# Fewer, wider segments in the second top-p search of a two-layer graph kernel

## The chip, the cores and the metric

The kernel runs on one core of one Trainium2 chip, in one launch, all in fp32. The metric is the device time of that launch in microseconds (us). TensorE is called PE below (PEld is its weight load), VectorE DVE, ScalarE ACT, GpSimd POOL and SyncE SP.

## The reference, cut to what matters

N is 2708 nodes with 256 features; adj is a sparse 2708 x 2708 matrix.

```python
x = layernorm(x + relu(concat([x, adj @ x]) @ weight + bias))          # layer 0
# layer 1
R = adj + eye(N);  R = R / R.sum(-1)
Xf = Xa = x;  Z = 0
for n in range(2):
    q = Xa @ W1.T @ W2.T;  k = Xa @ W3.T
    probs = softmax(q @ k.T)                     # N x N
    # of each row, keep the largest entries until their sum reaches TOP_P = 0.9
    idx = argsort(-probs);  sp = probs[idx];  cs = cumsum(sp)
    A = probs * (cs - sp < 0.9 at its place);  A = A / A.sum(-1)
    Xf = R @ Xf;  Xa = A @ Xa
    Z = Z + Xf @ U1[n].T + Xa @ U2[n].T
x = layernorm(x + layernorm(x + Z) * ln_g + ln_b)
```

Nothing is sorted over all 2708 entries of a row in the kernel. What it needs of a row is the threshold: the smallest entry that is kept.

## The kernel before, in words

The rows are cut into NB = 22 blocks of 128, the last (EDGE) with 20 rows. The work goes in three stages: layer 0; step 1 of the attention, together with a compaction of adj into at most 128 x 7 nonzero columns a block; and step 2 of the attention together with both products with R over the compacted columns. The change lies in step 2.

**Step 2, one block.** PE makes the logits in three parts (`logits`, L507); ACT takes their exponentials into a row buffer `e` (`exps2`, L844) and adds them up; DVE sums the three parts into the row's total z (`begin_search`, L852). Then a level is sought below which the threshold lies. The first level comes from a sum of square roots; for each level ACT goes over the row twice (`try_act`, L966 and L969, Relu and Sign with a running sum), which gives the mass and the number of entries above the level. `next_level` (L977) turns these into the next level with three constants of STEPS, and `last_level` (L1003 to L1013) picks one of two levels with the constant FEW. A row's level is thus a guess, made so that few entries stand between it and the threshold.

DVE finishes the row in this order:

- `below_level` (L1023): one pass that sets entries at or above the level to zero, into `low`, and adds up the rest;
- `candidates` (L1030): one MAX8 for each of NS2 segments of SEG2 elements of `low`, which gives the 8 largest of each segment, 160 candidates in `cand`;
- `in_order` (L1039, L1042): MAX8 and MATCH_REPLACE8 in turn, until TOP2 = 48 candidates stand in falling order in `srt`;
- `threshold` (L1058 to L1078): a running sum over these, the first that reaches the mass still needed, and how many entries equal to it are to be kept;
- `mark` (L1083): four MATCH_REPLACE8 of a quarter row, which mark these equal entries;
- `mask` (L1088): one pass that keeps what is above the threshold, in `e`.

PE then turns the masked row in six groups of up to four 128 x 128 transposes (`turn`, L527), ACT copies each group out of PSUM (L530), and PE multiplies (`products`, L564).

**The order of the work.** It is written out by hand as a loop over 24 periods with six slots each. In period `per` ACT tries the levels of block per + 1 and takes the exponentials of block per + 2; DVE does the level, `low` and candidates of block per, and the sorting, threshold, marks and mask of block per - 1; PE multiplies block per - 2, and does its share of the product with R (`r_units`, L749) in between. DVE's six slots are the generator `vector_slots`; `turns` deals out the steps of two generators alternately, so that a step which needs the result of the one before has others in front of it. The lines on which the edit acts are:

```python
run_all(turns((part_of_it(order, 7) if b else None, 1), (levels, 1)))   # slot 0
below_level(a)                                                          # slot 1
run_all(turns((order, 1), (part_of_it(cands, 8) if a else None, 2)))    # slot 2
run_all(turns((limits, 1), (cands, 2)))                                 # slot 3
mark(b, 0); mark(b, 1)                                                  # slot 4
mark(b, 2); mark(b, 3); run_all(begin); mask(b)                         # slot 5
```

Here a is block per and b is block per - 1. In the last two periods one or both are missing.

At the end of the program flags are added up: a row whose level was too low, whose threshold was not among the sorted candidates, or whose segment held more than 8 of the wanted entries sets one. If any is set, a branch runs `general_path`, which does the whole of layer 1 anew by another method.

Of the kernel before, what the change touches and what calls it, by code (L numbers as in the profile page):

```python
# [21 lines left out]
CH = 512  # L22
SEG = 170
NS = 16
SEG2 = 136
NS2 = 20
TOP1 = 64
TOP2 = 48
WS = 4

GUESS = 2.76141059
STEPS = ((0.93339875, 14.44678062, 82.55022771), (0.98700001, 8.00991560, 128.06811957))
FEW = 20.0
TOP_S = 0.8999
TIE_EPS = 1.5e-5
KS = 7
# [14 lines left out]
def gnn_two_layer_kernel(ctx: ExitStack, tc: tile.TileContext, N, xT_d, x_d, adj_d, w0_d, b0_d,  # L53
# [29 lines left out]
    assert N % 2 == 0 and NB % 2 == 0 and N * 2.0 ** -15 < 0.09 and DC == 2 and DA == 64  # L83
    assert SEG * (NS - 1) + 8 <= N <= SEG * NS == SEG2 * NS2 and N >= SEG2 * (NS2 - 1) + 8
    assert NB == 3 * KS + 1 and CW == P and CAP % 8 == 0 and N < NB * P
# [63 lines left out]
def fast_path(ctx, tc, c, flags, fint, xT_d, x_d, w0_d, b0_d, w1_d, w2_d, w3_d, u1_d, u2_d, g_d, b_d):  # L149
# [417 lines left out]
    def seg_max(dst, src, p, step, width):  # L567
        for i in range(NS):
            w = min(width, N - SEG * i) if step == SEG else width
            nc.vector.max(dst[:p, i * 8:(i + 1) * 8], src[:p, i * step:i * step + w])  # L570

    def put_in_order(dst, n, cand, p):

        spare = small.tile([P, NS2 * 8], FP, tag="spare", name="spare", bufs=1)[:, :cand.shape[1]]
        src = cand
# [11 lines left out]
    def extract1(t):  # L587
        p = rows(t)
        e = es[t % 4]
        cand = small.tile([P, NS2 * 8], FP, tag="cand", name="cand", bufs=2)[:, :NS * 8]  # L590
        seg_max(cand, e, p, SEG, SEG)
# [385 lines left out]
    def next_level(b, k):  # L977
        keep, slope, down = STEPS[k]
        nc.scalar.activation(b.kept, b.l[k], AF.Copy, scale=keep + TOP_P * slope, bias=-down)
        nc.scalar.activation((b.l1, b.l2)[k], b.u[k], AF.Identity, bias=b.kept, scale=-slope)  # L980
        if k:
            nc.scalar.activation(b.few, b.l1, AF.Copy, scale=TOP_P, bias=-FEW)

# [5 lines left out]
    def try_dve(b, k):  # L989
# [5 lines left out]
        if k == 0:  # L995
            keep, slope, down = STEPS[0]
            nc.vector.tensor_scalar(b.kept, b.l0, keep + TOP_P * slope, -down, op0=ALU.mult, op1=ALU.add)
# [20 lines left out]
    def below_level(b):  # L1018
# [5 lines left out]
                                       accum_out=bulk[:p, 2, t:t + 1])  # L1024
        b.cand = small.tile([P, NS2 * 8], FP, tag="cand", name="cand", bufs=2)

    def candidates(b):
        p = b.p
        for i in range(NS2):
            nc.vector.max(b.cand[:p, 8 * i:8 * i + 8], low[:p, SEG2 * i:SEG2 * (i + 1)])  # L1030
            yield

    def in_order(b):
        p = b.p
        b.srt = small.tile([P, TOP1 + 1], FP, tag="srt", name="srt", bufs=3)
        spare = small.tile([P, NS2 * 8], FP, tag="spare", name="spare", bufs=1)
        src = b.cand
        for i in range(0, TOP2, 8):
            nc.vector.max(b.srt[:p, i:i + 8], src[:p])  # L1039
            yield  # L1040
            if i + 8 < TOP2:
                nc.vector.match_replace(spare[:p], b.srt[:p, i:i + 8], src[:p], -3.0e38)  # L1042
# [3 lines left out]
    def threshold(b):  # L1046


        t, p = b.t, b.p
        s = b.srt[:p, :TOP2]  # L1050
        sc = small.tile([P, 3 + 2 * WS], FP, tag="sc", name="sc", bufs=3)
# [4 lines left out]
        x = sums  # L1056
        q_ = small.tile([P, TOP1], FP, tag="qs", name="qs", bufs=1)[:p, :TOP2]
        nc.vector.scalar_tensor_tensor(need, b.z, TOP_P - 1.0, below, op0=ALU.mult, op1=ALU.add)  # L1058
        nc.vector.tensor_tensor_scan(x[:p, 1:TOP2 + 1], s, s, 0.0, op0=ALU.add, op1=ALU.bypass)
        yield  # L1060
        nc.vector.scalar_tensor_tensor(q_, x[:p, 1:TOP2 + 1], need, s, op0=ALU.is_ge, op1=ALU.mult)
        yield
# [668 lines left out]
```

## Time and profile before

| what | us |
|---|---|
| median of 3 runs | 1310.96 |
| lowest and highest run | 1307.9, 1312.36 |
| the profiled execution | 1361.88 |
| its span, first to last instruction | 1360.1 |
| step 2, first `below_level` to the end | 779.0 to 1360.1 |

The profile is of one execution, at a mean granted TensorE clock of 0.969. All durations and places are on that execution's own time line. The rows of the edited lines on full blocks are: L1030, MAX8 of 128 x 136, 420 times, mean 286 ns; L1039, MAX8 of 128 x 160, 126 times, mean 316 to 319 ns; L1042, MATCH_REPLACE8 of 128 x 160, 105 times, mean 309 ns. Step 1 has the same operations in other widths: L570, MAX8 of 128 x 170, mean 320 ns; L577, MAX8 of 128 x 128, mean 284 to 295 ns; L579, MATCH_REPLACE8 of 128 x 128, mean 275 ns. A mean there is from the start of an instruction to the end of its write; the next instruction may start before that.

### The profile page before, as it was taken

What the parts mean: (1) busy time and instruction counts of PE and PEld (TensorE: products, weight loads), DVE (VectorE), ACT (ScalarE), POOL (GpSimd) and SP (SyncE); (2) the same over time, 40 slices, a digit from 0 to 9 for tenths busy, and PEclk for the clock granted to TensorE, in tenths of its full rate; (3) what the DMA queues carried; (4) which work ended last, traced back from release to release, by engine and by line L of the source; (5) the groups of instructions that cost most, each with busy time, mean ns of one, the idle gap of its engine ahead of it and who ended that gap; (6) DMA issues with size and microseconds to landing.
All of it is one profiled execution on the core that took longest, in us unless ns stands there. A gap on an engine that the chain in (4) does not pass through costs nothing.

```text
span 1360.1 us, 18883 instructions
## 1 busy us (share of the span) xinstructions
PE 1250.1 (92%) x5764; PEld 895.5 (66%) x5764; DVE 998.1 (73%) x3406; ACT 733.8 (54%) x1337; POOL 635.2 (47%) x594
## 2 busy tenths in 40 slices
PE   8999999988999999999997959999996999999985
PEld 6877877733567777666774727766664776666763
DVE  2544545866888888877840469878877899999995
ACT  1011011035455565555553577877786898998931
POOL 1000000014554533777563177777743668888850
PEclk9999999989899999999998969999998999999997
DMA  6554545513222110232222245645543444554541
GB/s 186 163 176 155 166 155 160 165 54 117 81 92 67 55 57 10 89 94 95 69 73 74 68 150 157 188 140 175 172 111 109 148 159 143 171 181 151 169 111 33
DMA packets 101993, 166.27 MB, mean 122 GB/s; under 512 B 17394, under 2 KB 74358, under 8 KB 101882
## 3 DMA queue, kind: packets, MB, share of 16 engines
q1 hardware_dynamic: 75596, 108.91, 24.7%
q0 software_dynamic: 20544, 51.17, 13.6%
q10 hardware_dynamic: 5742, 4.89, 1.3%
q8 instruction: 48, 0.79, 0.2%
q14 instruction: 63, 0.52, 0.1%
HBM read 130.87 MB, written 34.03 MB: 121 GB/s over the span
## 4 chain that ended last, share of the span: by engine, by line
PE 67%; ACT 19%; DVE 6%; issue 4%; another core or an unknown queue 2%; DMA 0%; ACTq 0%; DVEq 0%
PE acc L564 22%; PE acc L257 15%; PE lg L507 8%; PE tr L527 5%; PE misc L749 5%; ACT e L969 4%; ACT e L966 3%; ACT e L844 3%; ACT wT L530 3%; PE acc L651 2%; PE acc L462 2%; PE misc L426 2%; PE misc L392 2%; PE acc L672 2%
## 5 line engine op out<-in xcount | busy, mean ns | idle before, releaser
L530 ACT COPY wT<-tr 128x512 f32<-128x512 f32 (+2 forms) x258 | 131.7, 518 | 254.7 <-PE tr L527 153.3
L564 PE MATMUL acc<-ya,wT 128*128 128x256 f32 (+1 forms) x924 | 234.6, 394 | 18.8 <-ACT wT L530 12.1
L564 PE MATMUL acc<-x,wT 128*128 128x256 f32 (+1 forms) x924 | 234.6, 393 | 13.2 <-ACT wT L530 12.9
L719 POOL DMA_INDIRECT yg<-v_d,ix x154 | 190.1, 1234 | 79.4 <-issue 32.3
L564 PEld LDWEIGHTS acc<-x,wT 128*128 128x128 f32 (+1 forms) x924 | 167.2, 192 | 87.8 <-issue 40.6
L719 POOL DMA_INDIRECT yg<-yf_d,ix x154 | 192.6, 1250 | 62.3 <-issue 36.2
L564 PEld LDWEIGHTS acc<-ya,wT 128*128 128x128 f32 (+1 forms) x924 | 169.8, 193 | 75.6 <-issue 28.1
L257 PE MATMUL acc<-y,adj_t 128*128 128x257 f32 (+1 forms) x924 | 208.4, 381 | 0.0
L367 POOL DMA_INDIRECT adj_t<-in_adj,ix x154 | 170.3, 1106 | 51.4 <-issue 42.4
L749 PE MATMUL misc<-yg,adj_t 128*128 128x256 f32 (+1 forms) x704 | 183.5, 395 | 11.4 <-issue 6.6
L257 PEld LDWEIGHTS acc<-y,adj_t 128*128 128x128 f32 (+1 forms) x924 | 171.8, 189 | 32.7 <-issue 8.9
L507 PE MATMUL lg<-k,q 64*128 64x512 f32 (+3 forms) x528 | 151.9, 602 | 29.7 <-issue 11.2
L749 PEld LDWEIGHTS misc<-yg,adj_t 128*128 128x128 f32 (+1 forms) x704 | 125.7, 191 | 61.7 <-issue 31.2
L527 PE MATMUL tr<-ident,e 128*128 128x128 f32 (+2 forms) x946 | 147.0, 274 | 2.3 <-DVE e L1088 2.3
L527 PEld LDWEIGHTS tr<-ident,e 128*128 128x128 f32 (+2 forms) x946 | 113.6, 139 | 41.5 <-issue 17.6
L334 POOL DMA_DIRECT2D part_d<-e x1 | 0.6, 576 | 286.2 <-DVE e L333 286.2
L966 ACT ACTIVATE e<-e,st 128x2708 f32<-128x2708 f32 (+1 forms) x43 | 113.6, 2641 | 0.1
L570 DVE MAX8 cand<-e 128x8 f32<-128x170 f32 (+1 forms) x352 | 87.6, 318 | 32.7 <-ACT e L514 15.4
L969 ACT ACTIVATE e<-e,st 128x2708 f32<-128x2708 f32 (+1 forms) x42 | 110.9, 2641 | 0.1
L439 ACT COPY x1T<-tr 128x256 f32<-128x256 f32 (+1 forms) x22 | 8.0, 364 | 186.6 <-PE tr L438 186.6
L1030 DVE MAX8 cand<-w 128x8 f32<-128x136 f32 (+1 forms) x440 | 106.2, 285 | 0.0
L507 PEld LDWEIGHTS lg<-k,q 64*128 64x128 f32 (+1 forms) x528 | 39.3, 183 | 64.2 <-issue 35.6
(237 smaller groups left out, 1762.9 us busy)
## 6 DMA issues: line engine op xcount, KB each, us to landing
adj_t<-in_adj SPq DMA_DIRECT2D x44, 704.0 KB
adj_t<-adjc_d SPq DMA_DIRECT2D x44, 448.0 KB
adjc_d<-adj_t SPq DMA_DIRECT2D x22, 256.0 KB
base<-za_d SPq DMA_DIRECT2D x41, 128.0 KB
adjc_d<-adj_t SPq DMA_DIRECT2D x22, 192.0 KB
xt<-in_x ACTq DMA_DIRECT2D x21, 128.0 KB
x_d<-x SPq DMA_DIRECT2D x21, 128.0 KB
x1b_d<-xb SPq DMA_DIRECT2D x21, 128.0 KB
```

Source lines behind the costliest of these rows:

```text
L257: nc.tensor.matmul(acc[:p, :n], lhsT=halves[k // KH][:kw, k % KH, :p], rhs=y[:kw, k, :n], start=k == 0, stop=stop and k == NB - 1)
L367: nc.gpsimd.indirect_dma_start(out=a[:CW, i, :], out_offset=None, in_=adj_rows, in_offset=bass.IndirectOffsetOnAxis(ap=ix[:CW, m, i:i + 1] ...
L507: nc.tensor.matmul(lg[:p, h, :b - a], lhsT=q[o, t * P:t * P + p], rhs=keys[s][o, i, :b - a], start=True, stop=True)
L527: nc.tensor.transpose(tr[:kw, k % 4, :p], e[:p, k * P:k * P + kw], ident[:p, :p])
L530: nc.scalar.copy(wT[:, :full, :p], tr[:, :full, :p])
L564: nc.tensor.matmul(acc[:p, :D], lhsT=wT[:kw, k % 4, :p], rhs=y[:kw, k, :], start=k == 0, stop=k == NB - 1)
L570: nc.vector.max(dst[:p, i * 8:(i + 1) * 8], src[:p, i * step:i * step + w])
L719: nc.gpsimd.indirect_dma_start(out=y[:CW, i, :], out_offset=None, in_=rows_d, in_offset=bass.IndirectOffsetOnAxis(ap=ix[:CW, m, i:i + 1], ...
L749: nc.tensor.matmul(acc[:p, :D], lhsT=a[:kw, k, :p], rhs=y[:kw, k, :], start=k == 0, stop=k == CC)
L966: nc.scalar.activation(scr[:b.p, :N], e, AF.Relu, bias=b.nz, scale=b.l[k], accum_out=b.relu)
L969: nc.scalar.activation(scr[:b.p, :N], e, AF.Sign, bias=b.nz, scale=b.l[k], accum_out=b.sign)
L1030: nc.vector.max(b.cand[:p, 8 * i:8 * i + 8], low[:p, SEG2 * i:SEG2 * (i + 1)])
```

## The change

Step 2's candidates come from NS2 = 16 segments of SEG2 = 170 elements instead of 20 of 136, which is 128 candidates instead of 160, and TOP2 = 40 of them are put in order instead of 48. The constants by which the levels follow from one another are others. No function is edited; the loops and widths above follow from the constants. The row buffers stay 2720 elements wide (16 x 170 = 20 x 136), and a quarter row of `mark`, 680 elements, is four segments instead of five.

```diff
-SEG2 = 136
-NS2 = 20
+SEG2 = 170
+NS2 = 16
 TOP1 = 64
-TOP2 = 48
+TOP2 = 40
...
-STEPS = ((0.93339875, 14.44678062, 82.55022771), (0.98700001, 8.00991560, 128.06811957))
-FEW = 20.0
+STEPS = ((0.93305, 13.13978, 71.625), (1.02196, 8.0735, 138.42237))
+FEW = 18.8904
```

For a block, `candidates` issues 16 instead of 20 MAX8, `in_order` five MAX8 and four MATCH_REPLACE8 instead of six and five, and `threshold` the same operations on 40 and 128 elements instead of 48 and 160. In `vector_slots` slot 0 still takes seven steps of the sorting; two instead of four are left for slot 2, and eight instead of twelve candidate searches for slot 3.

## The prediction

> **What bounds the kernel now.** I read the page's busy shares first, then its chain of work, then the busy time by stage, then the chain and the timeline in two places: a steady period of step 2 and the end.
>
> ```profile
> PE 1250.1 (92%) x5764; PEld 895.5 (66%) x5764; DVE 998.1 (73%) x3406; ACT 733.8 (54%) x1337; POOL 635.2 (47%) x594
> PE 67%; ACT 19%; DVE 6%; issue 4%; another core or an unknown queue 2%; DMA 0%; ACTq 0%; DVEq 0%
> ```
>
> VectorE is busy for 73% of the span but holds 6% of the chain that ended last. The change edits VectorE alone, so the question is where that 6% lies. By stage (core, then length, then busy us of PE, PEld, DVE, ACT, POOL):
>
> ```profile
> 1151.56:1252.33 100.77, 95.08 (x443) 67.72 (x442) 94.35 (x343) 89.16 (x156) 83.36 (x73) 1.00 0.54 168
> 1252.33:1300.55 48.22, 44.35 (x219) 34.09 (x218) 46.27 (x166) 40.84 (x70) 39.91 (x36) 1.00 0.55 166
> 1300.55:1360.10 59.55, 39.30 (x221) 26.66 (x219) 45.14 (x146) 12.64 (x33) 11.71 (x12) 0.84 0.21 53
> ```
>
> The first row is four equal periods of 25.19 us. PE, DVE and ACT are all 88 to 94% busy, so busy time doesn't say which one sets the period. The chain and the timeline do (start, length, engine; in the timeline the idle time before is in brackets):
>
> ```profile
> 1190.24 0.48 ACT wT L530
> 1190.77 1.99 PE acc L564 x8
> ...
> 1199.03 1.99 PE acc L564 x8
> ...
> 1202.36 0.59 ACT wT L530
> ```
>
> ```profile
> 1194.66 0.16 DVE L852 TENSOR_REDUCE bulk<-st 128x1 f32<-128x3 f32 x1 [1.37 <-issue]
> 1202.36 0.59 ACT L530 COPY wT<-tr 128x512 f32<-128x512 f32 x1 [2.64 <-PE misc L749]
> ```
>
> The loop is ACT to PE to ACT: ACT's copy of turned weights releases eight matmuls, PE goes on to the next period's first transposes, ACT copies those after its only long pause, 2.64 us, and is then busy all period. No DVE piece stands in the chain from 779 to 1280 us. DVE pauses once a period, 1.36 us at L852, which sums what ACT's third exponential (L844, its accumulator read out at 1194.63) leaves. Its mask (L1088) ends at 1199.0; the transposes that need it start at 1201.73, so it is 2.7 us early. The second slack is larger than the first, so DVE work saved in a steady period becomes a longer pause at L852.
>
> The end is another matter. From L852 at 1270.18 to the end of the last mask at 1336.4 DVE has one pause, 0.11 us at L792, and the chain is on DVE from 1280.82:
>
> ```profile
> 1294.74 3.07 DVE e L1088 x2
> ...
> 1317.90 3.07 DVE e L1088 x2
> ...
> 1333.34 3.06 DVE e L1088 x2
> ...
> 1338.89 5.95 PE acc L550 x44
> ```
>
> ```profile
> 1321.11 0.63 PE L527 MATMUL tr<-ident,e 128*128 128x128 f32 x4 [2.28 <-DVE e L1088]
> ```
>
> No further exponentials are started there, ACT is busy for a fifth of the last stage, and PE waits 2.28 us for a mask. **Only here does saved DVE time shorten the run.**
>
> **What the Trainium skill says.** "Perfetto Trace Analysis", Optimizing Scalar/DVE Operations: a DVE operation on SBUF has about 60 ns of its own engine time, and the profiled latency is about twice the overhead, since the write acknowledgement overlaps the next instruction. So start-to-start time is the cost, not the listed mean. The trace agrees: 136 elements at 0.96 GHz ("VectorE: DVE Perf Modes", Specifications and errata table) and 60 ns give an estimate of 202 ns, and 20 MAX8 take (4.11 - 0.29)/19 = 201 ns each, though the row's mean is 286. The first page's section on the most-contended engine warns that matmul busy time is no measure of PE's distance from its limit; hence I go by pauses and the chain.
>
> ```profile
> 782.81 4.11 DVE L1030 MAX8 cand<-w 128x8 f32<-128x136 f32 x20
> 604.13 1.52 DVE L570 MAX8 cand<-e 128x8 f32<-128x170 f32 x6 [1.09 <-ACT e L514]
> 1321.82 0.32 DVE L1039 MAX8 srt<-spare 20x8 f32<-20x160 f32 x1
> 1322.58 0.32 DVE L1039 MAX8 srt<-spare 20x8 f32<-20x160 f32 x1
> 611.67 0.29 DVE L577 MAX8 srt<-spare 128x8 f32<-128x128 f32 x1
> 612.38 0.29 DVE L577 MAX8 srt<-spare 128x8 f32<-128x128 f32 x1
> ```
>
> **The change part by part**, for one row block. Step 1 already works with 170 and with 128 candidates, so its rows price the new shapes.
>
> *Candidates (L1030).* Before 20 x 0.203 = 4.06 us (0.201 alone, 0.205 between other steps). After 16 at 170 elements: step 1 has (1.52 - 0.32)/5 = 0.240, and 0.248 over a run of twelve; I take 0.244, 3.90 us. Gain 0.16 us; from 0.06 (at 0.250) to 0.27 (at 0.237).
>
> *Putting in order (L1039, L1042).* One MAX8, one MATCH_VALUE_LOAD and one MATCH_REPLACE8 fall away (six and five become five and four). Between other steps they occupy 0.23 + 0.29 = 0.52 us; with nothing between, as at 1321.82 to 1322.58, 0.76. The remaining nine are 32 elements narrower: 0.76 against step 1's 0.71 a pair gives 0.05 for each of 4.5 pairs, 0.22; by elements it would be 0.30. I take 0.25.
>
> *Threshold (L1058 to L1078).* Five operations on 40 instead of 48 and two on 128 instead of 160 save about 0.12 us by elements (bounds 0.05 and 0.2). But the steps are dealt out in turn: before, 4 sorting and 6 threshold steps had two candidate searches behind each; after, 2 and 4 have them, and L1071, L1073 lose their cover. Uncovered (block 21) L1071 to L1073 takes 0.34 and L1073 to L1075 0.24; covered, 0.22 and 0.12 to 0.19. Loss about 0.18 us (0.1 to 0.5, since L1061, L1064 and L1078 now and then take 0.65 to 0.75 in this trace).
>
> *Other constants.* They are immediates of the same instructions: no time. They do decide how many elements are left between level and threshold. Worked out with the formulas of L979, L980, L982 and L1003 to L1013 on the reference's input, the most any row needs is 34 elements (40 now kept) and 7 from one segment (8 kept), and no row's level lies past 0.9; so the branch to the general path stays untaken. Nothing is moved to another queue, and no DMA or semaphore wait on another engine is added.
>
> Sum for a covered block: 0.16 + 0.52 + 0.25 + 0.12 - 0.18 = 0.87 us; over 22 blocks some 19 us of DVE. For 19 of them the cover is DVE's own pause and the 2.7 us that the mask is early: nothing. After 1270.18 lie the sorting and threshold of blocks 19, 20 (covered, 0.87 each, with the searches of 20 and 21) and of 21 (no searches beside it: 0.76 + 0.25 + 0.12 = 1.13). Sum **2.87 us**. Does PE allow it? By the mask of block 20 it is 1.74, under PE's pause of 2.28. PE's own work for block 20 ends at 1335.2 and would end at 1333.5; the last mask would end at 1336.4 - 2.9 = 1333.5. Both are just met; PE is late next, so there is nothing beyond about 2.9 us. (The 0.11 us at L792 is put down to a matmul; if that holds, the 0.2 saved in front of it, in block 19's first sorting steps, is lost.)
>
> The profiled execution took 1361.88 us (span 1360.1), so 1359.0 is the sum against its own time. The median without profile is 1310.96, 51 us lower, with runs from 1307.9 to 1312.36; nothing in the end stage explains that difference, so I subtract the same 2.9: **1308.1 us**. That is 0.22%. About 0.3%, 3.9 us, is what a measurement of this kernel can tell from no change. The bounds (candidates 0.06 to 0.27, sorting 0.7 to 0.85, threshold -0.45 to 0.1) give 1 to 3.7 us.
>
> **The rivals.**
>
> *B, DVE is the bound in runs without profile.* If the ACT-PE loop is over 1.36 us shorter there, DVE sets every period and up to 19 us come off: 1292. For it: DVE is 94% busy, and plain runs are 51 us shorter. Against it: spread evenly, 51 us in 1361 is 0.94 us of a 25.19 us period, less than the pause; and the granted clock was already 1.00 in these periods, where the loop has least to gain. A partial form gives 4 to 10 us.
>
> *C, slower: stops that the trace puts down to no one.* In step 2 the chain has "another core or an unknown queue" at 796.3 (5.99 us), 810.2 (1.34), 907.7 (3.70), 989.4 (2.69), 1040.1 (4.54) and 1049.5 (0.97): 19.2 us, most of them before ACT instructions while DMA is heavy. 154 DVE instructions fewer move DVE against ACT and the transfers. Two further stops of the mean 3.2 us cost 6.4, less 2.9: 1314.5; at four, 1321. It decides from about seven added us. Against it: ACT's and PE's programs are unchanged, and the ACT-PE loop, not DVE, times them.
>
> *D, nothing comes out.* If the uncovered threshold steps cost 0.5 and PE or the gathered rows (PE waits 1.15 us for yg at 1312.65) hold the end: under 1 us, 1310.5.
>
> **How the numbers follow.** Main case 0.60: 1308.1, own range 1306.5 to 1310; with the scatter of medians I read it as within 0.3% for 0.44 of these and as faster for 0.16. B 0.22, faster. C 0.13, slower. D 0.05, within 0.3%. Faster 0.16 + 0.22 = 0.38, within 0.3% 0.44 + 0.05 = 0.49, slower 0.13. The range 1298 to 1314 takes in the partial form of B and leaves out its full form and the worse half of C.
>
> **What would show it.** Right: DVE's count falls by 154 to 3252; MAX8 at L1030 x352 near 320 ns; the pause at L852 in steady periods grows from 1.36 to about 2.2 while periods stay at 25.2; the stretch from the last L852 to the end of the last mask shrinks from 66.2 to about 63.4 us. Wrong: steady periods shorter than 25 us without a new clock (B), new unattributed stops on ACT or DVE (C), a PE pause before the last L544 that is released by matmuls (D).

## The result, and the profile after

The changed kernel takes **6518.32 us** (median of 6 runs, 6510.56 to 6522.13), the kernel before 1309.43 us (6 runs beside them, 1305.68 to 1312.36): a ratio of 4.9755, with a 95% interval from 4.9651 to 4.9858. The forecast was 1308.1 us, with a range from 1298 to 1314.

The page of the kernel after shows that a second program has run behind the first. Its lines are engine, busy us, share of the span and number of instructions, then the chain that ended last by engine, and the costliest group (count, busy us, mean ns, idle time before it):

```profile
span 6508.8 us, 37828 instructions
PE 2881.0 (44%) x11676; PEld 1998.5 (31%) x11676; DVE 5929.0 (91%) x8620; ACT 1347.3 (21%) x2298; POOL 749.3 (12%) x682
DVE 77%; PE 17%; ACT 3%; issue 2%; DMA 0%; SPq 0%; POOL 0%; DVEq 0%; ACTq 0%; POOLq 0%
L1516 DVE SCALAR_TENSOR_TENSOR scr<-e,cand 128x2708 f32<-128x2708 f32 (+1 forms) x1188 | 3630.1, 3056 | 49.7 <-ACT e L1495 4.1
```

L1516 stands in `general_path`. It has no row in the profile of before; here it runs 1188 times, which is 2 steps x 22 blocks x 27 passes of 3.06 us over whole rows, and is over half of the span. The chain is now on DVE for 77%.

Where the second program begins is seen in SP's queue and in the chain of waits (start, length, what):

```profile
1299.77 10.28 SPq L1424 DMA_DIRECT2D x<-x_d  x22
```

```profile
1297.88 0.42 DVE h L1190
1298.72 0.51 SPq L127
...
1310.48 7.08 DMA adj_t<-in_adj
...
1400.02 3.06 DVE scr L1516 x2
1403.18 3.06 DVE scr L1516 x2
```

L127 reads the sum of the flags. The last layer norm of the ordinary path (L1190) ends at 1298.3, where the kernel before would have been done but for its last stores; at 1299.77 L1424 loads x again for `general_path`. From there to the end are 6508.8 - 1299.8 = 5209.0 us, and the medians differ by 6518.32 - 1309.43 = 5208.9. **The loss is the branch at the end; none of it that could be seen lies in the search.**

Ahead of the branch the profile can be laid beside that of before. Busy time by stage (start and end, length, busy us of PE, PEld, DVE, ACT, POOL, granted clock, DMA share, GB/s), each stage at the same distance from the last L852 as before:

```profile
1099.95:1200.64 100.69, 95.01 (x442) 67.77 (x441) 91.08 (x313) 89.17 (x156) 82.32 (x73) 1.00 0.55 168
1200.64:1248.86 48.22, 44.36 (x219) 34.20 (x218) 45.39 (x151) 41.35 (x72) 39.66 (x36) 1.00 0.55 167
1248.86:1299.70 50.84, 39.23 (x221) 27.92 (x219) 43.67 (x134) 12.14 (x32) 10.90 (x12) 0.87 0.24 59
```

```profile
1142.95 0.16 DVE L852 TENSOR_REDUCE bulk<-st 128x1 f32<-128x3 f32 x1 [2.10 <-ACT e L844]
1150.66 0.59 ACT L530 COPY wT<-tr 128x512 f32<-128x512 f32 x1 [2.64 <-PE tr L527]
```

Four steady periods take 100.69 us where they took 100.77, though DVE is busy for 91.08 and not 94.35. The timeline says why: DVE's pause at L852 has grown from 1.37 to 2.10 us, and ACT's pause of 2.64 us stands as it was.

### The profile page after: what moved, and what is told of

It is laid out like the page before. It is cut to its first block, busy times and chain, and to the rows that moved or that the text cites. A ratio compares the mean times of both kernels' runs of the same rounds, so it can differ in the third digit from the quotient of the medians.

```text
span 6508.8 us, 37828 instructions
## 1 busy us (share of the span) xinstructions
PE 2881.0 (44%) x11676; PEld 1998.5 (31%) x11676; DVE 5929.0 (91%) x8620; ACT 1347.3 (21%) x2298; POOL 749.3 (12%) x682
## 4 chain that ended last, share of the span: by engine, by line
DVE 77%; PE 17%; ACT 3%; issue 2%; DMA 0%; SPq 0%; POOL 0%; DVEq 0%; ACTq 0%; POOLq 0%
DVE scr L1516 56%; PE acc L564 5%; DVE scr L1539 4%; PE acc L257 3%; DVE e L1544 2%; DVE scr L1542 2%; DVE scr L1532 2%; DVE nmax L1486 2%; PE lg L507 2%; DVE cand L1518 2%; DVE th L1519 1%; DVE cand L1512 1%; PE misc L749 1%; PE tr L527 1%; DVE scr L1538 1%
## 5 line engine op out<-in xcount | busy, mean ns | idle before, releaser
L1516 DVE SCALAR_TENSOR_TENSOR scr<-e,cand 128x2708 f32<-128x2708 f32 (+1 forms) x1188 | 3630.1, 3056 | 49.7 <-ACT e L1495 4.1
L1569 PE MATMUL tr<-ident,e 128*128 128x128 f32 (+1 forms) x968 | 180.1, 317 | 3004.0 <-DVE e L1544 2982.2
L1417 PE MATMUL acc<-v,adj_t 128*128 128x256 f32 (+1 forms) x968 | 261.9, 437 | 435.8 <-DMA adj_t<-in_adj 432.5
L1478 PE MATMUL lg<-qk 64*128 64x512 f32 (+1 forms) x528 | 335.2, 802 | 59.4 <-ACT e L1480 59.4
L1417 PEld LDWEIGHTS acc<-v,adj_t 128*128 128x128 f32 (+1 forms) x968 | 206.3, 217 | 490.3 <-issue 450.7
L1560 PE MATMUL acc<-ya,wT 128*128 128x256 f32 (+1 forms) x968 | 282.5, 444 | 2.7 <-ACT wT L1572 2.5
L1539 DVE TENSOR_TENSOR_SCAN scr<-scr,before 128x1354 f32<-128x1354 f32 (+1 forms) x88 | 267.4, 3038 | 3.1
L1560 PE MATMUL acc<-x,wT 128*128 128x256 f32 (+1 forms) x968 | 254.3, 409 | 2.0 <-ACT wT L1572 2.0
L564 PE MATMUL acc<-ya,wT 128*128 128x256 f32 (+1 forms) x924 | 234.1, 393 | 12.6 <-ACT wT L530 12.3
L564 PE MATMUL acc<-x,wT 128*128 128x256 f32 (+1 forms) x924 | 230.6, 389 | 0.0
L1417 PE MATMUL acc<-yf,adj_t 128*128 128x256 f32 (+1 forms) x968 | 227.5, 395 | 0.0
L1417 PEld LDWEIGHTS acc<-yf,adj_t 128*128 128x128 f32 (+1 forms) x968 | 183.6, 193 | 42.4 <-issue 13.6
```

What stands on the lines that cost most here:

```text
L564: nc.tensor.matmul(acc[:p, :D], lhsT=wT[:kw, k % 4, :p], rhs=y[:kw, k, :], start=k == 0, stop=k == NB - 1)
L1417: nc.tensor.matmul(acc[:p, :n], lhsT=halves[k // KH][:kw, k % KH, :p], rhs=y[:kw, k, :n], start=k == 0, stop=stop and k == NB - 1)
L1478: nc.tensor.matmul(lg[:p, :b - a], lhsT=qk[o, 0, t * P:t * P + p], rhs=qk[o, 1, a:b], start=True, stop=True)
L1516: nc.vector.scalar_tensor_tensor(scr[:p, 0, :], e[:p], cand[:p, j:j + 1], e[:p], op0=ALU.is_ge, op1=ALU.mult, accum_out=mass[:p, j:j + 1])
L1539: nc.vector.tensor_tensor_scan(run, eq, eq, before[:p], op0=ALU.add, op1=ALU.bypass)
L1560: nc.tensor.matmul(acc[:p, :D], lhsT=wT[:kw, k - k0, :p], rhs=y[:kw, k, :], start=k == 0, stop=k == NB - 1)
```

## The experiments

Three theories were to be told apart. **T1:** one row is at fault: it needs more than 40 sorted entries and sets a flag. **T2:** the wider segments are at fault: one of 170 holds more than 8 wanted entries. **T3:** the new levels are at fault: a row's level is too low. Beside it, what does the change do to the ordinary path? Each comparison is with runs of the kernel before on the same chip; the chip of the four kernels e1 to e4 has a median of 1356.92 us for it, those of the others 1309.48 and 1309.5.

**e1_sort48.** The change, with 48 entries put in order.

```diff
-TOP2 = 40
+TOP2 = 48
```

> The changed kernel with 48 candidates put in order again; segments and constants stay changed. Theory 1 (one row's threshold lies beyond its 40th candidate; with the first level taken from columns 0 to 1023, row 2634 needs 43): no flag, the general path isn't entered, about 1308 us. Theory 2 (a segment of 170 holds more than 8 wanted entries) and theory 3 (a level lies past 0.9 with the new constants): the flag stays, about 6515 us. If theory 1 holds, the time of the fast path against before: segments alone save 0.16 us of DVE a block, so -0.5 us, no difference that can be measured.

1354.56 us (the expected 1308 belongs to a chip on which before takes 1311), ratio 0.9979 (0.9957 to 1.0001). The branch isn't taken, with the new segments and the new constants in place. T2 and T3 fall: the count of 40 is what sets the flag.

**e3_after_over1.** The change, with the branch taken only if more than one flag is set.

```diff
-with tc.If(again > 0)
+with tc.If(again > 1)
```

> The changed kernel, whose branch enters the general path at two flags or more instead of one: row 2634 then keeps more entries than it should, and the rest is the changed kernel's own fast path. Theory 1 says that exactly one flag is set: the path isn't entered, and the time is that of the changed fast path, 1308 us by the sum of the prediction (2.9 us off before; the last L852 to the end of the last mask 64.6 us, as in the changed profile, against 66.2). Theories 2 and 3, with flags in several rows: about 6515 us.

1354.98 us, ratio 0.9987 (0.9968 to 1.0006). So exactly one flag is set. The run also gives the time of the changed ordinary path alone: not measurably different from before. Its interval is wide: it holds the forecast 0.9978 as well as 1, so e3 alone doesn't decide on the 2.9 us.

**e4_after_rows_cleared.** The change, with the flags of 32 rows of block 20 (rows 2624 to 2655) set to zero in the test of the kept mass alone.

```diff
+nc.vector.memset(flags[64:96, 4 * NB + 20:4 * NB + 21], 0.0)
 nc.vector.tensor_reduce(flags[:, 5 * NB:6 * NB], bulk[:, 5:, :]...
```

> The changed kernel with the test of kept mass left out for 32 rows, 2624 to 2655 (block 20, partitions 64 to 95), by one small memset; all other tests stay. Theory 1, which names row 2634 and this test: the general path isn't entered, about 1308 us. If another test or another row sets the flag: about 6515 us.

One run, 1356.1 us, no second program. The one flag is in these 32 rows and in the test of L1338: what the mask keeps is not what the running sum over the sorted entries accounts for. The run leaves 32 rows. Worked out with the kernel's formulas on the reference's input it is row 2634, whose threshold is its 43rd largest entry below the level; no other of the 32 needs more than 40.

**e2_sort40_alone_over1** and **e7_sort40_alone_over2.** The kernel before with 40 entries put in order, old segments and old constants; branch at more than one flag, then at more than two.

```diff
-TOP2 = 48
+TOP2 = 40
-with tc.If(again > 0)
+with tc.If(again > 1)          # e7: again > 2
```

> The kernel before with 40 instead of 48 put in order and nothing else changed, and its branch entered at two flags or more. Theory 1: with the old constants rows 215 and 2634 need 48 and 43, so two flags are set and the general path is entered, about 6515 us. Theories 2 and 3: no flag, about 1308 us.

> The kernel before with 40 put in order alone, and its branch entered at three flags or more; up to two rows then keep more entries than they should. Theory 1 (rows 215 and 2634, one flag each): not entered, so with the same kernel at two flags or more the count is exactly two; the time of the fast path, a few us around before. If more rows are flagged: about 6560 us.

e2 takes 6564.94 us, e7 1311.49 (one run each), so the old constants with 40 set exactly two flags. That is what the formulas give: with the old constants two rows need more than 40, row 2634 with 43 and row 215 with 48. The runs count the flags; which rows they are is worked out. The page of e2 carries the same group as that of after:

```profile
span 6563.2 us, 37916 instructions
L1516 DVE SCALAR_TENSOR_TENSOR scr<-e,cand 128x2708 f32<-128x2708 f32 (+1 forms) x1188 | 3630.5, 3056 | 49.7 <-ACT e L1495 4.1
```

The new constants bring row 215 down to 35, but leave row 2634 at 43. They do shorten the longest list, only not far enough for the new count. By the same formulas row 215 had filled all 48 places of the kernel before, which thus stood at its limit.

**e8_fitted40** and **e9_fitted32.** The change with constants that are fitted to this one input, so that the largest need is 32, or 31, and with 40 or 32 entries put in order.

```diff
-STEPS = ((0.93305, 13.13978, 71.625), (1.02196, 8.0735, 138.42237))
-FEW = 18.8904
+STEPS = ((0.97673, 13.88523, 62.44572), (1.00441, 11.34134, 113.55263))   # e8
+FEW = 15.80857
+STEPS = ((0.95236, 12.94316, 56.68032), (1.02438, 12.71254, 135.62837))   # e9, TOP2 = 32
+FEW = 19.70188
```

> The changed kernel with other level constants, fitted to this input with the first level's sum over the right columns, so that no row needs more than 32: STEPS ((0.97673, 13.88523, 62.44572), (1.00441, 11.34134, 113.55263)), FEW 15.80857. Theory 1: no flag, and the time of the changed fast path, ratio 0.9978 by the prediction's sum (2.9 us); if the DVE work saved in the steady periods counted as well, 0.986 (19 us). Theories 2 and 3 say nothing certain of it.

> As the kernel with fitted constants, but 32 put in order, with constants for which no row needs more than 31: STEPS ((0.95236, 12.94316, 56.68032), (1.02438, 12.71254, 135.62837)), FEW 19.70188. Theory 1: no flag. Another pair of sorting steps falls away, 0.5 us a block covered, 0.75 in the last one: some 0.6 to 1.8 us less than with 40 if DVE sets only the end, since PE's own work is met there; 11 us less if DVE set every period.

No branch in either. e8: 1309.77 us, ratio 1.0003 (0.9989 to 1.0016). This is the change as it was meant to be, and it is no faster: the prediction's 2.9 us, 0.9978, lie outside the interval. e9: 1305.12 us, ratio 0.9977 (0.9964 to 0.9990), the one kernel of these that is measurably faster than before, by 0.1 to 0.4%. It is 4.65 us faster than e8, where 0.6 to 1.8 were expected. The constants of both hold for this input only.

**e5_segments_alone** and **e6_constants_alone.** The kernel before with one part of the change each.

```diff
-SEG2 = 136
-NS2 = 20
+SEG2 = 170                      # e5; e6 has the new STEPS and FEW instead
+NS2 = 16
```

> The kernel before with 16 segments of 170 instead of 20 of 136, 48 put in order and the old constants. Theory 1: no flag; DVE saves 0.16 us a block and some 0.1 on the narrower sort, so no difference that can be measured (ratio 0.998 to 1.001). Theory 2: a flag, about 6560 us.

> The kernel before with the new STEPS and FEW alone. Theory 1: no flag and the time of before, as they are immediates of the same instructions. Theory 3: a flag, about 6560 us.

e5: 1309.34 us, ratio 1.0002 (0.9989 to 1.0015). e6: 1306.36 us in one run, with steady periods and masks as before. Neither takes the branch, so each of the two parts is harmless alone.

**e10_sort64.** The change with 64 entries put in order, three more MAX8 and three more MATCH_REPLACE8: to see what happens once DVE's pause is used up.

```diff
-TOP2 = 40
+TOP2 = 64
```

> The changed kernel with 64 put in order instead of 40: three more MAX8, MATCH_VALUE_LOAD and MATCH_REPLACE8 a block, 1.5 us of DVE where other steps cover them, 2.1 in the last block. No flag. If DVE has 1.4 us to spare before and about 2.2 after the change in each steady period, these stay at 25.2 us, the pause at L852 there falls to about 0.7, and the last L852 to the end of the last mask grows by 4 to 5 us: ratio 1.001 to 1.003. If DVE sets the periods: 19 times 1.5 us more, ratio 1.02.

1312.03 us, ratio 1.0020 (1.0009 to 1.0032). Four steady periods:

```profile
1127.50:1228.20 100.70, 93.61 (x438) 67.02 (x437) 98.72 (x348) 89.10 (x157) 82.90 (x73) 1.00 0.54 167
```

```profile
1143.98 0.15 DVE L852 TENSOR_REDUCE bulk<-st 128x1 f32<-128x3 f32 x1
```

DVE is busy for 98.72 of 100.70 us, and the period is still 25.2. The pause at L852 is gone altogether, where 0.7 us of it was expected to be left: the three pairs cost 2.14 us a period in the table below, not 1.5. The loss of 2.5 us against 1309.5 is that of the last stage: from the last L852 to the end of the last layer norm 83.1 us, against 80.6 in e6. The last mask comes 3.7 us later than in e8; 4 to 5 were expected.

**What the ordinary path gained.** DVE's time for the three slots that hold the sorting, the candidates and the threshold, start to start, in a steady block (us, from the timelines); then the pause at L852; then, from the last L852 on, when the masks of blocks 20 and 21 end, and the time from the mask of block 20 to the end of the last layer norm:

| kernel | slots 0, 2, 3 | sum | pause | mask 20 | mask 21 | mask 20 to end |
|---|---|---|---|---|---|---|
| constants alone (e6), the instructions of before | 2.65, 2.66, 5.04 | 10.35 | 1.36 | 50.77 | 66.21 | 29.86 |
| segments alone (e5) | 2.42, 2.81, 4.84 | 10.07 | 1.64 | 50.31 | 65.50 | 29.82 |
| the change, 40 (e8) | 2.41, 2.36, 4.84 | 9.61 | 2.10 | 50.23 | 64.89 | 29.83 |
| the change itself | 2.41, 2.36, 4.84 | 9.61 | 2.10 | 49.96 | 64.58 | 29.84 |
| 32 sorted (e9) | 2.42, 1.90, 5.26 | 9.58 | 2.12 | 49.70 | 63.09 | 26.97 |
| 64 sorted (e10) | 2.42, 4.11, 5.22 | 11.75 | 0 | 52.26 | 68.63 | 30.88 |

The last column is the point. In e6, e5, e8 and after it is the same within 0.04 us, although the mask of block 21 comes up to 1.6 us earlier: in these four executions the chain behind the mask of block 20 is PE's. The chain of e8 (start, length, what) shows it:

```profile
1265.30 3.07 DVE e L1088 x2
1268.50 0.98 PE tr L527 x4
...
1272.53 3.23 PE acc L564 x8
...
1276.20 1.73 PE acc L564 x8
...
1282.48 2.78 PE acc L564 x12
1285.26 1.34 PE tr L544 x22
```

From 1268.5 on no DVE piece stands in it until PE has multiplied block 21. Here only the mask of block 20 counts, and that came 50.77 - 50.23 = 0.54 us earlier in e8, 0.81 in after. 0.5 of 1309.5 us is 0.04%, too little for e8 to tell from nothing.

e9 falls out of the column by 2.9 us. Here the granted clock differs, in the first 8 us behind the mask of block 20 (first two rows e8, then e9, the columns as above):

```profile
1268.35:1272.35 4.00, 3.85 (x13) 2.58 (x14) 3.46 (x18) 1.97 (x4) 0.00 (x0) 0.53 0.04 9
1272.35:1276.35 4.00, 4.00 (x15) 3.27 (x15) 3.75 (x17) 0.84 (x3) 1.49 (x2) 0.61 0.42 131
```

```profile
1269.10:1273.10 4.00, 3.87 (x21) 2.98 (x22) 3.68 (x18) 1.98 (x4) 0.00 (x0) 1.00 0.04 11
1273.10:1277.10 4.00, 3.87 (x22) 3.27 (x21) 3.81 (x17) 1.82 (x4) 1.53 (x2) 1.00 0.42 131
```

With the clock at 0.53 and 0.61 e8 gets 28 matmuls done where e9, at 1.00, does 43. The clock alone doesn't give e9's 2.9 us, though. e7 (40 sorted, old segments and old constants) had a clock of 1.00 there too, for 16 us, and still needed 29.82 us from the mask of block 20 to the end; the low clock came later, during L550:

```profile
1272.50:1276.50 4.00, 3.87 (x21) 2.98 (x22) 3.74 (x17) 1.75 (x4) 0.00 (x0) 1.00 0.03 6
1284.50:1288.50 4.00, 3.23 (x27) 2.40 (x25) 3.88 (x7) 0.39 (x2) 0.00 (x0) 1.00 0.00 0
1288.50:1292.50 4.00, 3.40 (x41) 1.83 (x43) 3.56 (x15) 0.57 (x2) 0.00 (x0) 0.69 0.27 80
```

```profile
1269.43 3.07 DVE e L1088 x2
...
1284.35 3.06 DVE e L1088 x2
1287.40 0.14 issue
1287.54 1.50 PE tr L544 x22
...
1289.63 4.99 PE acc L550 x44
```

Its chain runs on DVE from the mask of block 20 to that of block 21, as in the profile of before, and L550 takes 4.99 us where it takes 3.30 in e8 at a clock of 1.00. In these profiles the chain goes with the place of the low clock: it is PE's where the clock falls right behind the mask of block 20 (e3, at 0.68 and then 0.89, has 28.20 us there), and DVE's where it falls behind that of block 21. e9 has no low clock until L550 is done, and its mask of block 21 comes 3.1 us earlier than in e6. How its 2.9 us divide between these two, one execution doesn't tell. Its 0.9977 in plain runs is measured. Of these, 9 of 15 had a mean clock of 0.981 or more, with a median of 1304.14 us; of before's 36 runs beside them 11 had, with 1306.50. So some 2.4 of the 4.4 us remain at a like mean clock; the rest goes with a clock that is lowered less.

## Why the prediction was wrong

**The step that failed is "Other constants".** It says that "the most any row needs is 34 elements (40 now kept)" and that "the branch to the general path stays untaken". Right is 43, in row 2634. The first level comes from a sum of square roots, and `exps2` (L848) writes the square roots into columns 1024 to 2047 of the row buffer; the prediction's working took these for the columns that are summed. What L848 reads is `lg` of the first part, columns 0 to 1023; the place of the output is only scratch. The code in question:

```python
if i == 0:      # lg is the first part of the logits
    nc.scalar.activation(e2(b.t)[:b.p, HC:2 * HC], lg, AF.Exp, bias=b.half, scale=0.5, accum_out=b.roots)
```

With the right columns the old constants need 48 at most and the new ones 43. e1 (48: no flag), e3 (exactly one), e4 (where) and the pair e2, e7 (exactly two with the old constants) agree with these numbers. Taken with columns 1024 to 2047, the same formulas give the prediction's 34 for the new constants and 40 for the old ones; neither the change nor e2 would then have set a flag, and both did. What the flag does then: the sum over 40 entries doesn't reach the mass that is still needed, the threshold stays at zero, the mask keeps more than it should, L1338 sees it, and one row of 2708 sends the whole of layer 1 through the other method.

**The rivals left it out.** A flag was treated as excluded by that one piece of arithmetic, so the general path had no chance and no price. The price couldn't be read in the profile of before, in which it never runs, but a bound could: the general path does the same products again, and with 27 passes of 3.04 us (L1023's pass over a row) for each of 44 row blocks comes to 3600 us at least. As the rival on the slower side it would have stood thousands of us away, where C stood at 1321, 10 us above before.

**What held.** "DVE work saved in a steady period becomes a longer pause at L852" is shown: periods of 25.2 us throughout, the pause from 1.36 to 2.10 us (forecast: about 2.2), ACT's pause unchanged. DVE's count falls by the 154 foretold, from 3406 to 3252 in e3 and e8. e10 shows the same from the other side: 2.14 us more of DVE's work fill the pause of 2.10 and leave the period as it was. What more than the pause would cost, no run tried.

**Sizes.** For a covered block 0.87 us was forecast, 10.35 - 9.61 = 0.74 was measured. Segments, candidates and narrower sorting together give 10.35 - 10.07 = 0.28, where the terms "Candidates" and the 32 elements narrower had 0.16 + 0.25; the eight entries fewer give 10.07 - 9.61 = 0.46, all in slot 2, where 0.52 stood. The price of a MAX8 at 170 was not the fault: six take 1.42 us in the chain of after (`1252.84 1.42 DVE cand L1030 x6`), 0.237 each, which is the same estimate that held at 136: about 60 ns of DVE's own time (the Trainium skill, "Perfetto Trace Analysis", Optimizing Scalar/DVE Operations) and 170 elements at 0.96 GHz ("VectorE: DVE Perf Modes", Specifications).

**The last stage, "both are just met".** This term was mis-sized most. The mask of block 20 was to come 1.74 us earlier and the last mask 2.87, and the end with it. In e8 the first came 0.54 us earlier and the last 1.32 (0.81 and 1.63 in after), and the end only with the first. Two things are seen. Some of the threshold's small steps stretch: in e8's chain

```profile
1232.03 0.73 DVE qs L1061
...
1233.37 0.84 DVE qs L1064 x2
...
1236.28 0.47 DVE part L1078
```

L1061 does so with two searches ahead of it, so lost cover isn't the whole reason; what is, no run tells. The slot with the threshold of block 20 takes 5.78 us in after where it took 5.49. And PE is late next, as the prediction says, but much sooner than at 2.9 us: at a granted clock of 0.5 to 0.6 its work behind the mask of block 20 leaves no room at all. The profile of before, on which the term rests, had a clock of 1.00 there, and the mask of block 21 in its chain, as e7 has. In e9, also at 1.00 there but with the earliest masks, the chain is PE's from 4.7 us behind the mask of block 20 on. The term took the clock of one execution for that of all.

**The other rivals.** B, DVE as the bound of plain runs with up to 19 us to gain, falls: e8 at 1.0003 and e10 at 1.0020 both lie where the last stage puts them. The 51 us on which B leaned are no cost of profiling: on the chip of e1 to e4 plain runs of before have a median of 1356.92 us, and on the others profiled executions take 1305 to 1312. Of C, new stops before ACT, nothing was seen beyond a scatter: from the first L1023 to the last L852 e6 has 461.9 us, e8 and after 463.3, e5 463.4, e7, e9 and e10 464.0 to 464.3. Whether these 1.4 to 2.4 us are the edits or the one execution of e6 stays open; they are more than the 0.54 us gained behind them. D, "nothing comes out", is what the change would have been without the flag.

## What to carry to other kernels

A limit that guards a fallback is no tuning constant like the others: work out its largest use row by row from the operands that the code reads, and price the fallback with its condition as a case of its own, however unlikely. Where the sorting of 48 was exactly full (row 215), any smaller number is a change of what the kernel does, not of how fast it does it. An engine at 94% busy that wasn't on the chain gave nothing back here: look for the pause that grows, and in the last stage for the piece after which another engine holds the chain, in more than one execution.

## What the runs showed of the hardware

- The granted TensorE clock fell for some 8 us in the last stage of these executions, and not always at the same place: behind the mask of block 20 in e5, e6, e8 and after (0.5 to 0.64), behind that of block 21 in e7 (0.69). PE's work stretched with it: eight matmuls of L564 took 3.23 us in e8's chain in the low stretch and 1.73 at 1.00. In the general path, where PE is busy for about a third of the time, the clock was 0.62.
- The stretch from the first L1023 to the last L852 took 483.8 to 491.1 us in the four profiles on the chip whose median is 1356.92, and 461.9 to 464.3 in the six on the chips of 1309.5. e3 and e8, which differ in the constants alone there, have 491.1 and 463.3. Such a difference goes with the chip, and no edit was read from it.
- Small DVE steps are uneven: L1061 took 0.28 us on 128 x 64 in a block of e10, and 0.81 on 128 x 40 in the block of e8 shown above (0.73 of it in the chain).
